# Stage 4 of a four-stage sequence model on one core: query norms inside the exponential, output projection over two tiles, norm bias folded into the first product's bias

## The chip, the cores and the metric

One core of a Trainium2 chip runs the whole program. The metric is the device time of an execution in microseconds (us). The kernel before takes 2695.79 us as the median of three runs (2693.87 to 2695.86).

## The reference, cut to what matters

The program takes 2048 tokens of width 128 through four residual stages. Only the last, a stack of six layers, is touched. The input of that stage is layer-normed first. In each layer, shift_tokens moves the upper 64 features one token on.

```python
def attn_layer(x, Wqkv, qs, ksc, Wo):                # 16 heads of 64
    q, k, v = split(x @ Wqkv)
    q = l2norm(q) * qs;  k = l2norm(k) * ksc         # per head
    q, k = rotary(q, scale), rotary(k, 1 / scale)
    out = local_attention(q, k, v)                   # windows of 32, each sees itself and the one before
    return out @ Wo
def local_attention(q, k, v):
    sim = einsum('bhwie,bhwje->bhwij', bq, bk2) * 8.0
    attn = softmax(where(mask, -max, sim))           # 64 columns per row
    return einsum('bhwij,bhwje->bhwie', attn, bv2)
def ffn_layer(x, g, bln, W1, b1, W2, b2):
    xn = (x - mu) / sqrt(var + 1e-5) * g + bln
    a, gate = split(xn @ W1 + b1)                    # 341 columns each
    return a * gelu(gate) @ W2 + b2
for i in range(6):
    x = attn_layer(shift_tokens(x), ...) + x
    x = ffn_layer(shift_tokens(x), ...) + x
```

## The kernel before, in words

Stage 4 works on tiles of 128 tokens: 16 tiles a layer, 96 in six layers. The residual lies transposed in SBUF (features in partitions), in two buffers s4[0] and s4[1]. All data are 32-bit floats.

One loop, `for i in range(last + 2 * G + len(parts))`, is a software pipeline. In each pass it calls the list `steps` in the order written, and each step has a lag: `(mix, 4)` works in pass i on tile i - 4. The engines keep the program's order, because every call goes through `InOrder` (this is why nearly all lines in the profile are L66, the helper's). So in each pass ACT, for instance, runs in this order: the square of Q (sq), the copy of V (vt), the exponential (ex), what the feed-forward step needs, the square of K (sq again), and four copies out of PSUM (qT, kT, pT, oT).

The steps of one tile are these. `project` multiplies by the weights of Q or K into ps (PE) and squares it (ACT). `rotate` makes the two rotary terms rot_a and rot_b out of ps (DVE), `rotate_sum` adds them (POOL), `squares` sums sq by head into ss (DVE). `norms` raises ss to the power -1/2 (POOL, rn: the inverse norms of Q in rn[:, 0] and of K in rn[:, 1]); `normed` multiplies K by its norms (POOL). `turn` transposes Q and K (PE into pt, ACT copies to qT and kT). `scores` makes sc out of a mask and 64 small products (PE). `shift` takes the row maximum mx, subtracts it (DVE, sm) and multiplies by the norms of Q (POOL, sm again). `expo` is the exponential (ACT, ex). `project_v` makes the values (PE into pv, ACT copies to vt, and DMAs on SP's queue spread vt over the windows of vw). `flip` transposes ex (PE into ptp, ACT copies to pT). `weigh` multiplies by the values (PE into po) and divides by the row sum (DVE, rd and o). `turn_o` transposes o (PE into pto, ACT copies to oT), `mix` multiplies by the output weights (PE into px), and `take` adds px to the residual (DVE, two halves of 64 partitions because of the shift).

The feed-forward part works on groups of four tiles (512 columns), cut in seven `parts`, of which a pass runs those with index p = i mod 4 and p + 4: ff_mean with the second of three products ff_up, ff_var with the third, ff_norm with ff_down, and the first ff_up alone. ff_mean makes xc and its square xsq, ff_norm spreads the inverse deviation over PSUM (prb) and normalises, ff_up makes ph (PE), the GELU ge (ACT) and the gated act (DVE).

PSUM is one pool of four buffers of two banks each; `big` hands them out to all of the products named above, and a product waits until the one that had its buffer has been read. The pool `wk` holds twelve SBUF tiles of 128x1024 for sq, rot_b, sm, ex, qT, pT, o and oT.

The exponential and the GELU use different tables on ACT; the compiler puts a table load ahead of an instruction whose table isn't in place.

Of the kernel before, what the change touches and what calls it, by code (L numbers as in the profile page):

```python
# [11 lines left out]
F32 = mybir.dt.float32  # L12
BF16 = mybir.dt.bfloat16
I32 = mybir.dt.int32
AF = mybir.ActivationFunctionType
ALU = mybir.AluOpType
# [3 lines left out]
P = 128  # L20
T = 2048
NT = T // P
# [12 lines left out]
DEPTH = 6  # L35
# [3 lines left out]
NPAIR = HEADS // 2  # L39
WIN = 32  # L40
NWIN = P // WIN
QK_SCALE = 8.0
FFI = 341
FCH = [(0, 128), (128, 128), (256, 85)]
# [6 lines left out]
def _bc(ap, shape):  # L51

    return ap.unsqueeze(len(shape) - 1).to_broadcast(shape)
# [30 lines left out]
class Kernel:  # L84
# [722 lines left out]
    def stage4(self, x3T, out):  # L807
        nc, tc, a = self.nc, self.tc, self.a
        with ExitStack() as ctx:
            self.pools4.append(ctx.enter_context(tc.tile_pool(name="s4w1", bufs=1)))  # L810
            const = ctx.enter_context(tc.tile_pool(name="s4c", bufs=1))
            pool = ctx.enter_context(tc.tile_pool(name="s4", bufs=2))
            pool3 = ctx.enter_context(tc.tile_pool(name="s43", bufs=3))
            wk = ctx.enter_context(tc.tile_pool(name="s4wk", bufs=12))
            psum = ctx.enter_context(tc.tile_pool(name="s4b", bufs=4, space=PSUM))


# [5 lines left out]
            vec = const.tile([P, DEPTH, 9], F32, name="vec4")  # L823
# [29 lines left out]
            for g in range(NG):  # L853
                cols = slice(g * GW, (g + 1) * GW)
                xc = pool.tile([P, GW], F32, name="xc")
                pr = self.norm_columns(xc, x3T[:, cols], mean_w, pool, psum)
# [6 lines left out]
            pe, dve, act, gps, sp = self.pe, self.dve, self.act, self.gps, InOrder(tc, nc.sync)  # L863
            st = [{} for _ in range(DEPTH * NT + 1)]
            ff = [{} for _ in range(DEPTH * NG)]

            def big(name):
                return psum.tile([P, 2, 512], F32, name=name, tag="big")
# [139 lines left out]
            def shift(t):  # L1008
                s_ = st[t]
                sc = s_.pop("sc").rearrange("p h n k -> p (h n) k")  # L1010
                mx = pool.tile([P, HEADS], F32, name="mx4")
                dve.reduce_max(mx, sc, axis=AX.X)
                sm = wk.tile([P, HEADS, 2 * WIN], F32, name="sm", tag="wk")
                dve.tensor_tensor(sm, sc, _bc(mx, [P, HEADS, 2 * WIN]), ALU.subtract)

                gps.tensor_tensor(
                    sm.rearrange("p (h n) k -> p h n k", h=2),
                    sm.rearrange("p (h n) k -> p h n k", h=2),
                    _bc(s_.pop("rn")[:, 0, :].rearrange("p (n h) -> p h n", h=2), [P, 2, NPAIR, 2 * WIN]),
                    ALU.mult,  # L1020
                )
                s_["sm"] = sm

            def expo(t):
                s_ = st[t]
                sm = s_.pop("sm")
                ex = wk.tile([P, NPAIR, 2, 2 * WIN], F32, name="ex4", tag="wk")
                act.activation(
                    ex.rearrange("p n h k -> p h n k"), sm.rearrange("p (h n) k -> p h n k", h=2), AF.Exp
                )  # L1030
                s_["ex"] = ex

            def flip(t):
# [38 lines left out]
            def turn_o(t):  # L1072
                o = st[t].pop("o")
                pt = big("pto4").rearrange("p a (n c) -> p (a n) c", c=P)
                for n in range(NPAIR):
                    pe.transpose(pt[:, n, :], o[:, n].rearrange("p h d -> p (h d)"), self.ident)
                oT = wk.tile([P, NPAIR, P], F32, name="oT", tag="wk")
                act.copy(oT, pt)
                st[t]["oT"] = oT

            def mix(t):
                wo = self.w4[t // NT][1]
                oT = st[t].pop("oT")
                px = big("px4")[:, 0, 0:P]
                for n in range(NPAIR):
                    pe.matmul(px, lhsT=wo[:, n, :], rhs=oT[:, n, :], start=n == 0, stop=n == NPAIR - 1)
                st[t]["px"] = px

            def take(t):
                i, px = t % NT, st[t].pop("px")  # L1090
                for h in range(2):
                    rs = slice(64 * h, 64 * h + 64)
                    cols = slice(i * P + h, (i + 1) * P + h)
                    dve.tensor_tensor(s4[1][rs, cols], s4[0][rs, cols], px[rs], ALU.add)


# [23 lines left out]
            def ff_norm(g):  # L1120
                xc, r, vc = ff[g]["xc"], ff[g].pop("r"), vec[:, g // NG]
                pr = big("prb")[:, 0]
                for j in range(G):
                    pe.matmul(
                        pr[:, j * P : (j + 1) * P], lhsT=r[:, j : j + 1].to_broadcast([P, P]), rhs=self.ident,
                        start=True, stop=True,
                    )
                dve.tensor_tensor(xc, xc, pr, ALU.mult)
                dve.tensor_scalar(xc, xc, vc[:, 0:1], vc[:, 1:2], ALU.mult, ALU.add)

            def ff_up(g, i):
                (c0, cn), xc, vc, w1 = FCH[i], ff[g]["xc"], vec[:, g // NG], self.w4[g // NG][2]
# [13 lines left out]
            def ff_down(g):  # L1146
# [12 lines left out]

            parts = [  # L1160
                ff_mean, ff_var, ff_norm, lambda g: ff_up(g, 0), lambda g: ff_up(g, 1), lambda g: ff_up(g, 2), ff_down
            ]

            def feed_forward(i):
# [6 lines left out]

            steps = [
                (lambda t: project(t, 0), 0), (mix, 4), (lambda t: rotate(t, 0), 0), (take, 4), (scores, 2),
                (lambda t: squares(t, 0), 0), (shift, 2), (normed, 1), (lambda t: rotate_sum(t, 0), 0), (table, -1),
                (project_v, 2), (expo, 2), (weigh, 3), (feed_forward, None),
                (lambda t: project(t, 1), 0), (turn, 1), (lambda t: rotate(t, 1), 0), (lambda t: rotate_sum(t, 1), 0),
                (pass_on, 1), (lambda t: squares(t, 1), 0), (flip, 2), (turn_o, 3), (norms, 0),
            ]
            last = DEPTH * NT
            table(0)  # L1180
            for i in range(last + 2 * G + len(parts)):
                if i % NT == 12 and i // NT + 1 < DEPTH:
                    self.load4(i // NT + 1)
                for step, late in steps:
                    if late is None:
                        step(i)
                    elif 0 <= i - late < last:
                        step(i - late)
# [141 lines left out]
```

## Time and profile before

| | us |
|---|---|
| median of three runs | 2695.79 |
| the profiled execution | 2700.82 |
| its span, first to last instruction | 2699.1 |
| PE, DVE, ACT, POOL busy in the span | 2459.0, 1821.7, 1349.7, 1658.8 |
| PE, DVE, ACT, POOL busy in 1900 to 2200 us | 286.1, 223.7, 168.5, 268.6 |
| exponential of stage 4, 96 of 128x1024, each | 1.057 |
| POOL's multiply of sm by the norms, 96, each | 1.911 |
| px, 1536 matmul records of 128 columns, each | 0.280 |
| table loads on ACT, 133, each | 1.283 |

The profile is of one execution, 5.0 us above the median. A row gives the number of instructions, their busy time and the mean duration of one; a product of 32-bit floats appears as two records. Records of PE overlap their neighbours, so the distance from start to start is the better measure of what a matmul costs. Stage 4 begins at about 900 us. A busy share is an average: it doesn't tell which engine the next step is waiting for.

### The profile page before, as it was taken

Reading aid. Unit: us, or ns where it says so; the run is one execution under the profiler, and the core shown is the slowest. Engines: PE = TensorE matmul, PEld = TensorE weight load, DVE = VectorE, ACT = ScalarE, POOL = GpSimd, SP = SyncE. Lnnn points to the kernel's source line nnn. Section 1 sums busy time; section 2 is a strip of 40 time slices with the busy share of each in tenths; the row PEclk is TensorE's granted clock in tenths of the full one; section 3 lists DMA queues with packets and bytes.
Section 4 is the critical chain, followed back from the end, with each engine's and each line's share of the span. In section 5 each row is a group of like instructions: output and inputs, shape, how many; then the busy total and the mean of one; then the engine's idle time right before and its main releaser. Section 6 shows DMA issues by size and latency. Waiting matters only on the chain.

```text
span 2699.1 us, 85362 instructions
## 1 busy us (share of the span) xinstructions
PE 2459.0 (91%) x37600; PEld 1478.4 (55%) x37600; DVE 1821.7 (67%) x2764; ACT 1349.7 (50%) x1806; POOL 1658.8 (61%) x1011
## 2 busy tenths in 40 slices
PE   3489999999999689999999999999999999999997
PEld 1473333333333366666666666666666666666664
DVE  6766664476642467777777777777777777777774
ACT  1132455544555144555555555555555555556552
POOL 4310000000001599989888888898888988898980
PEclk8689999999999799999999999999999999999999
DMA  2000000000000222233222322232323222222221
GB/s 82 1 1 1 1 1 1 2 1 1 1 1 1 62 65 69 60 88 72 59 66 67 89 58 71 66 87 60 73 62 82 69 66 67 59 60 65 60 59 43
DMA packets 93566, 128.39 MB, mean 48 GB/s; under 512 B 26248, under 2 KB 41104, under 8 KB 93072
## 3 DMA queue, kind: packets, MB, share of 16 engines
q1 hardware_dynamic: 92620, 122.48, 18.6%
q8 instruction: 299, 4.90, 0.8%
q10 hardware_dynamic: 580, 0.46, 0.1%
q14 instruction: 67, 0.55, 0.1%
HBM read 20.35 MB, written 1.05 MB: 8 GB/s over the span
## 4 chain that ended last, share of the span: by engine, by line
PE 63%; DVE 21%; ACT 6%; issue 5%; POOL 4%; SPq 1%; DMA 0%; DVEq 0%; ACTq 0%; POOLq 0%
PE sc L66 17%; PE ps L66 10%; PE av L66 6%; PE pt L66 5%; DVE mx L66 4%; PE py L66 4%; DVE rot_a L66 4%; DVE sm L66 4%; DVE ss L66 4%; PE ph L66 3%; DVE rot_b L66 3%; PE pto L66 3%; PE ptp L66 3%; ACT sq L66 3%; POOL sm L66 2%
## 5 line engine op out<-in xcount | busy, mean ns | idle before, releaser
L66 DVE TENSOR_REDUCE mx<-sc 128x1 f32<-128x512 f32 (+4 forms) x736 | 471.0, 685 | 238.9 <-PE sc L66 234.1
L66 POOL TENSOR_TENSOR rot_a<-rot_a,rot_b 128x1024 f32<-128x1024 f32 x192 | 459.2, 2392 | 144.1 <-DVE rot_b L66 143.9
L66 POOL TENSOR_TENSOR rn<-ss,mhalf 128x32 f32<-128x32 f32 x96 | 523.9, 5457 | 8.0
L66 ACT ACTIVATE ex<-sc 128x512 f32<-128x512 f32 (+3 forms) x640 | 310.0, 531 | 302.4 <-PE sc L66 301.3
L66 PE MATMUL sc<-kT,qT 64*32 64x64 f32 (+2 forms) x13568 | 429.7, 260 | 9.6 <-ACT qT L66 9.3
L66 POOL TENSOR_SCALAR_AFFINE_SELECT ex<-ex 128x512 f32<-128x512 f32 x64 | 40.6, 634 | 628.2 <-ACT ex L66 628.2
L66 DVE TENSOR_TENSOR rot_a<-ps,tab 128x1024 f32<-128x1024 f32 x192 | 235.0, 1224 | 221.9 <-ACT sq L66 205.3
L66 PE MATMUL sc<-qT,kT 32*128 32x512 f32 (+3 forms) x1280 | 369.4, 581 | 2.3 <-DVE qT L66 2.1
L66 PE MATMUL ps<-wqkv,s 128*128 128x512 f32 x768 | 367.8, 602 | 1.5 <-DVE rd L66 1.5
L66 ACT COPY vt<-pv 128x1024 f32<-128x1024 f32 x96 | 97.2, 1013 | 443.4 <-PE pv L66 425.4
L66 PEld LDWEIGHTS sc<-kT,qT 64*32 64x32 f32 (+1 forms) x13568 | 221.5, 113 | 139.1 <-issue 68.9
L66 ACT ACTIVATE sq<-ps 128x1024 f32<-128x1024 f32 x192 | 195.9, 1020 | 101.4 <-PE ps L66 101.4
L66 DVE TENSOR_REDUCE ss<-sq 128x16 f32<-128x1024 f32 x192 | 233.1, 1214 | 2.8
L66 DVE TENSOR_TENSOR rot_b<-ps,tab 128x1024 f32<-128x1024 f32 x192 | 233.0, 1213 | 0.0
L66 PEld LDWEIGHTS pt<-ident,rot_a 128*128 128x128 f32 x1536 | 175.5, 142 | 76.8 <-issue 40.3
L66 PEld LDWEIGHTS px<-oT,wo 128*128 128x128 f32 x1536 | 182.3, 193 | 63.5 <-ACT oT L66 61.4
L66 PEld LDWEIGHTS ps<-wqkv,s 128*128 128x128 f32 x768 | 138.6, 191 | 141.5 <-issue 136.7
L66 ACT ACTIVATE ex<-sm 128x1024 f32<-128x1024 f32 x96 | 101.5, 1057 | 221.2 <-POOL sm L66 221.2
L66 PE MATMUL pt<-ident,rot_a 128*128 128x128 f32 x1536 | 188.3, 275 | 23.3 <-POOL rot_a L66 23.1
L66 POOL TENSOR_TENSOR sm<-sm,rn 128x1024 f32<-128x1024 f32 x96 | 183.5, 1911 | 40.6 <-DVE rd L66 18.7
L66 DVE SCALAR_TENSOR_TENSOR act<-ph,vec,ge 128x512 f32<-128x512 f32 (+1 forms) x72 | 54.0, 750 | 220.1 <-ACT ge L66 220.0
L66 PE MATMUL px<-oT,wo 128*128 128x128 f32 x1536 | 194.9, 280 | 6.7 <-ACT oT L66 6.7
(212 smaller groups left out, 4014.2 us busy)
## 6 DMA issues: line engine op xcount, KB each, us to landing
vw<-vt SPq DMA_DIRECT2D x1524, 65.0 KB, 2.0
wqkv<-in_L_ffn_Wqkv SPq DMA_DIRECT2D x18, 512.0 KB, 5.1
wo<-in_L_ffn_Wo SPq DMA_DIRECT2D x6, 512.0 KB, 4.7
w<-in_L_ffn_W SPq DMA_DIRECT2D x6, 341.0 KB, 3.3
x<-in_L_attn_hidden_states SPq DMA_DIRECT2D x4, 256.0 KB, 4.3
rot<-in_rot SPq DMA_DIRECT2D x1, 1024.0 KB
out<-ot SPq DMA_DIRECT2D x4, 256.0 KB, 2.2
w<-in_L_ffn_W SPq DMA_DIRECT2D x12, 64.0 KB, 2.6
```

The lines of the kernel that those rows point to most:

```text
L66: return self._tc.keep_in_program_order(call(*args, **kw))
```

## The change

`shift` no longer multiplies by the norms of Q. `expo` becomes 16 instructions, one for each head, on 64 columns each, and each gives its head's column of rn as the scale of the exponential: exp(rn * (sc - mx)). rn is positive, so the maximum stays the maximum.

`turn_o` copies into one half of an oT that two tiles share, out of a pool of its own with two buffers. `mix` and `take` do nothing for an even tile; for an odd one they work on both (256 columns).

`ff_norm` multiplies by g and by prb in one step and leaves out the bias. A new function, `ff_bias`, called once in each layer ahead of the steps of pass i with i mod 16 = 6, makes the product of that bias with W1 (six products with one column) and adds it to b1. `wk` goes from twelve tiles to ten.

```diff
-            wk = ctx.enter_context(tc.tile_pool(name="s4wk", bufs=12))
+            wk = ctx.enter_context(tc.tile_pool(name="s4wk", bufs=10))
...
                 dve.tensor_tensor(sm, sc, _bc(mx, [P, HEADS, 2 * WIN]), ALU.subtract)
-
-                gps.tensor_tensor(
-                    sm.rearrange("p (h n) k -> p h n k", h=2),
-                    sm.rearrange("p (h n) k -> p h n k", h=2),
-                    _bc(s_.pop("rn")[:, 0, :].rearrange("p (n h) -> p h n", h=2), [P, 2, NPAIR, 2 * WIN]),
-                    ALU.mult,
-                )
                 s_["sm"] = sm
...
-                sm = s_.pop("sm")
+                sm, rn = s_.pop("sm"), s_.pop("rn")
                 ex = wk.tile([P, NPAIR, 2, 2 * WIN], F32, name="ex4", tag="wk")
-                act.activation(
-                    ex.rearrange("p n h k -> p h n k"), sm.rearrange("p (h n) k -> p h n k", h=2), AF.Exp
-                )
+
+                for n in range(NPAIR):
+                    for h in range(2):
+                        act.activation(
+                            ex[:, n, h, :], sm[:, h * NPAIR + n, :], AF.Exp, scale=rn[:, 0, 2 * n + h : 2 * n + h + 1]
+                        )
...
-                oT = wk.tile([P, NPAIR, P], F32, name="oT", tag="wk")
-                act.copy(oT, pt)
-                st[t]["oT"] = oT
+                if t % 2 == 0:
+                    st[t + 1]["oT"] = pool.tile([P, NPAIR, 2, P], F32, name="oT")
+                oT = st[t + 1 - t % 2]["oT"]
+                act.copy(oT[:, :, t % 2], pt)
...
             def mix(t):
+                if t % 2 == 0:
+                    return
...
-                px = big("px4")[:, 0, 0:P]
+                px = big("px4")[:, 0, 0 : 2 * P]
                 for n in range(NPAIR):
-                    pe.matmul(px, lhsT=wo[:, n, :], rhs=oT[:, n, :], start=n == 0, stop=n == NPAIR - 1)
+                    pe.matmul(
+                        px, lhsT=wo[:, n, :], rhs=oT[:, n].rearrange("p j c -> p (j c)"), start=n == 0, stop=n == NPAIR - 1
+                    )
...
             def take(t):
-                i, px = t % NT, st[t].pop("px")
+                if t % 2 == 0:
+                    return
+                i, px = t % NT - 1, st[t].pop("px")
...
-                    cols = slice(i * P + h, (i + 1) * P + h)
+                    cols = slice(i * P + h, (i + 2) * P + h)
...
-                dve.tensor_tensor(xc, xc, pr, ALU.mult)
-                dve.tensor_scalar(xc, xc, vc[:, 0:1], vc[:, 1:2], ALU.mult, ALU.add)
+
+                dve.scalar_tensor_tensor(xc, xc, vc[:, 0:1], pr, ALU.mult, ALU.mult)
+
+            def ff_bias(l):
+                w1, vc = self.w4[l][2], vec[:, l]
+                pb = big("pbias")[:, 0, 0:6]
+                for h in range(2):
+                    for i, (c0, cn) in enumerate(FCH):
+                        pe.matmul(
+                            pb[0:cn, 3 * h + i : 3 * h + i + 1], lhsT=w1[:, h * FFI + c0 : h * FFI + c0 + cn],
+                            rhs=vc[:, 1:2], start=True, stop=True,
+                        )
+                for i, (_, cn) in enumerate(FCH):
+                    dve.tensor_tensor(vc[0:cn, 3 + i : 9 : 3], vc[0:cn, 3 + i : 9 : 3], pb[0:cn, i:6:3], ALU.add)
...
+                if i % NT == 6 and i // NT < DEPTH:
+                    ff_bias(i // NT)
```

## The prediction

> **What bounds the kernel now.** I read the page first: the last two thirds of the span (stage 4) have PE at 9 tenths, POOL at 8 to 9, DVE at 7, ACT at 5. That looks like a kernel bound by PE, with ACT half idle. The waits by engine (window 1500 to 2500 us, about 55 tiles) show where ACT's idle time sits:
>
> ```profile
> ACT vt L66 <- PE pv L66: 240.8, 52, 5.2
> ACT ex L66 <- POOL sm L66: 120.8, 55, 3.3
> PEld px L66 <- ACT oT L66: 33.3, 55, 0.7
> ```
>
> PE's own waits are small, and ACT waits twice in each tile: for pv, and for POOL's multiply. Next the timeline of one pass of the loop, ACT alone, in a pass that also runs a feed-forward product (columns: start, time taken, instruction, idle time before it):
>
> ```profile
> 2044.29 1.03 ACT L66 ACTIVATE sq<-ps 128x1024 f32<-128x1024 f32 x1 [0.24 <-PE ps L66]
> 2049.95 1.01 ACT L66 COPY vt<-pv 128x1024 f32<-128x1024 f32 x1 [4.63 <-PE pv L66]
> 2050.98 1.28 ACT L66 ACT_TABLE_LOAD   x1
> 2054.06 1.06 ACT L66 ACTIVATE ex<-sm 128x1024 f32<-128x1024 f32 x1 [1.79 <-POOL sm L66]
> 2055.02 0.61 ACT L66 ACTIVATE xsq<-xc 128x512 f32<-128x512 f32 x1
> 2055.65 1.28 ACT L66 ACT_TABLE_LOAD   x1
> 2056.94 0.69 ACT L66 ACTIVATE ge<-ph,vec 128x512 f32<-128x512 f32 x1
> 2057.53 1.02 ACT L66 ACTIVATE sq<-ps 128x1024 f32<-128x1024 f32 x1
> 2058.43 1.01 ACT L66 COPY qT<-pt 128x1024 f32<-128x1024 f32 x1
> 2059.32 1.04 ACT L66 COPY kT<-pt 128x1024 f32<-128x1024 f32 x1
> 2060.23 1.04 ACT L66 COPY pT<-ptp 128x1024 f32<-128x1024 f32 x1
> 2061.13 1.06 ACT L66 COPY oT<-pto 128x1024 f32<-128x1024 f32 x1
> 2062.44 1.02 ACT L66 ACTIVATE sq<-ps 128x1024 f32<-128x1024 f32 x1 [0.25 <-PE ps L66]
> ```
>
> The reader is to see that from ex to oT ACT has no idle time, and that the next sq comes only 0.25 us after it could. Between the first sq and ex lies DVE: rot_a, rot_b, take, ss, mx, sm in one string, sm ending 7.75 us after the first sq began. So there is a ring, sq, DVE's string, POOL's multiply, ex, ACT's string, sq, that is as long as PE's work (18.15 us here). PE and this ring bound the stage together; whatever lengthens the ring shows in full, whatever shortens only one of the two shows hardly at all.
>
> **What the Trainium skill says.** "ScalarE: Activation LUTs", section What ACT_TABLE_LOAD costs: an instruction costs 186 ns + 0.833 ns a column, a pointer operand adds about 93 ns, neighbours overlap by about 93 ns, a table load takes 1283 ns. The trace agrees: loads 1283 ns; ge (bias by pointer, 512 columns) 687 ns against 590 ns of a copy of that size; ge begins 0.58 us before the next, 0.1 less than it takes. "TensorE: Matmul & The Clock Gate", section Part 1: The HAM clock gate: PE's activity is judged in free windows of 3.4 us, and after an idle one PE runs at half clock. In the trace's tail, where PE has gaps of 0.55 and 1.76 us close together, the same px takes 3.45 us in place of 1.95 to 2.05:
>
> ```profile
> 2638.71 3.45 PE L66 MATMUL px<-oT,wo 128*128 128x128 f32 x16 [1.76 <-ACT oT L66]
> ```
>
> **The change, part by part.** Times are counted from S, the start of the pass's first sq. I name passes by i mod 4: a (2: norm and down), b (3: up 0), c (0: mean and up 1), d (1: variance and up 2). The timeline from 2008 us has them as a 18.56, b 17.69, c 18.15, d 17.70, together 72.1.
>
> *The exponentials.* One ex of 1057 ns becomes 16 of 128x64 with a scale by pointer. The trace has no such row. From its rows: 1057 less 960 columns at 0.833 is 257 ns, plus 97 for the pointer (687 against 590) is 354 ns; neighbours overlap by about 0.1 (ex starts 0.96 before xsq). So about 0.25 us each, 4.0 us for 16. Bounds: 0.354 without overlap (5.7 us); 0.12 if start and pointer both hide, worked out from stage 3, where a second 128-column exponential adds only 0.175 us (0.107 of columns, 0.068 fixed):
>
> ```profile
> 664.90 0.45 ACT L66 ACTIVATE ex<-sc 128x128 f32<-128x128 f32 x2 [1.40 <-PE sc L66]
> L66 ACT ACTIVATE ex<-sc 128x128 f32<-128x128 f32 x64 | 14.3, 275 | 29.3 <-PE sc L66 29.1
> ```
>
> I take 0.25, because a pointer showed its full price behind ge.
>
> *POOL's multiply* (1.91 us) leaves the ring: ex may start when sm ends, not 2.0 later. But part of this is lost. In the built order the wait for sm now stands ahead of the table load on ACT, where before the load had no wait and ran while POOL multiplied. In c, d and a, which load the exponential's table, 1.28 us become visible; b loads none. So c's first ex starts at S+8.5, against S+9.8. Behind that wait stand, in ACT's order, the 16 exponentials, ge, sq and the four copies, and for these wait act and ptp (ge), DVE's next rot_a (sq), pto (qT), ps (kT) and px (oT).
>
> *Two tiles at once.* px of 16 matmul records at 0.11 us becomes, in odd passes (b, d), 16 at 0.215 (a 512-column record of ps is 0.43), 3.44 us, and nothing in a and c. PE's sum is the same but for 0.07 us a tile. The placing is not: in b and d, sc and pv come 1.65 later and the vt copy, ahead of ex on ACT, ends at S+8.43 instead of S+6.67. DVE's take is gone in a and c (0.6 us, sm ends S+7.12) and 0.83 in b and d (sm ends S+8.13, take waiting for px until S+3.5).
>
> *The walk round the ring*, with ACT's own spacings (ex to load 4.1, load 1.30, ge 0.58, sq 0.91, qT 0.89, kT 0.90, pT 0.90, oT 1.07; xsq 0.63 more in c):
> - a: first ex S+8.47, sq at S+12.47 (ps has been ready since S+11.5), next S at 17.15: 1.41 less.
> - b: ex S+8.45, next S at 19.1: 1.41 more.
> - c: ex S+8.47, next S at 19.65: 1.50 more.
> - d: vt S+8.43, load, ex S+9.75, next S at 20.4: 2.70 more.
>
> Sum +4.2 us in four passes. In each, ps for the next S needs the kT copy and ends within 0.1 of oT, so PE gives no relief. Products of the feed-forward lie beside attention in 22 such rounds (passes 11 to 97): 22 x 4.2 = 92. The nine passes before them go from 16.25 to a mean of 16.45: +2.
>
> *Half clock.* In c PE has finished pt at S+12.35, and ptp must take the buffer that act frees after ge: S+16.0. An idle stretch of 3.6 us is new; before it was 0.2. At half clock one window costs up to 1.7 us of PE work, and ps is on the path. Bounds 0 and 37 us over 22 rounds (1.7 each); I take 1.0 each, 22.
>
> *The bias product.* Six one-column products a layer, 12 records at 0.11 to 0.12 (pvar's 8 take 0.9), ahead of ps at i mod 16 = 6, where ps is on the path: 1.4 x 6 = 8. They also hold a PSUM buffer until three small DVE additions, which run while DVE waits for sq. *The norm*: xc's two DVE steps (0.68 and 1.89) become one of 0.75. Worth nothing: DVE then idles 1.1 us before rot_a for sq. *Buffers 12 to 10*: oT has its own pair now; the new waits in the built order (qT and pT copies for POOL's sums) are for sums that end at S+12 at the latest, before those copies. Nothing; SP's DMAs are unchanged.
>
> Sum 92 + 2 + 22 + 8 = 124, onto the profiled execution's 2700.8: 2825. The median stands 5 below that execution, so **2820**.
>
> **The rivals.**
> - *Cheap exponentials, faster.* The place is the 16 instructions between sm and ge. At 0.12 us they take 1.94: b, c, d gain 2.06 each on my walk and a 1.0 (ps at S+11.5 then ends last): 4.2 - 7.2 = -3.0 a round, -65, with 10 for bias and first passes and no half clock: -55, 2641. It decides from 0.173 us each downwards (3.7 us a round to be found in b, c and d: 1.23 less than 4.0). For it: the 0.068 of stage 3. Against: ge's pointer shows 0.1, and SBUF sources cost 37 ns more than PSUM ones (1057 against 1020).
> - *Exponentials without overlap.* 5.66 us: 1.66 more in all four passes, 146 more: 2966. Against: every back-to-back pair on ACT overlaps by 0.1.
> - *Half clock spreads.* The window after c's stall falls on d's long px: 1.7 more a round, 37: 2857. For: the tail's px. Against: d's px comes over 3 us after the stall.
> - *PE alone bounds*, and the ring's time is covered: then only 0.07 x 96 = 7 us of px less 8 of bias: 2697. Against: the next sq waits only 0.25 us.
>
> **How the numbers follow.** About 0.2% is what a measurement of this kernel can tell from no change. My walk 0.66, half clock spreading 0.14, no overlap 0.08, cheap exponentials 0.09, PE alone 0.03. The range, 2745 (exponentials near 0.2 us, no half clock) to 2900 (0.30 us with half clock), holds the first two and leaves out the last three, 0.20 together. Faster 0.09, same 0.03, slower 0.88.
>
> **What would show it.** In the changed profile: ex rows of 128x64 near 350 ns starting 0.25 apart; a table load directly after sm in c, d and a; no idle time on ACT from there to oT; PE waiting for act before ptp, by 3 us in c; passes b and d longer than a; clock below 1.0 inside stage 4. It is wrong if ACT still waits before ge, or if the exponentials stand 0.17 apart or closer.

## The result and the profile after

The changed kernel takes 2812.65 us (median of four runs, 2808.81 to 2814.19) against 2695.82 in the same comparison: 116.8 us more, ratio 1.0431 with a 95% interval of 1.0413 to 1.0449. The forecast was 2820, in a range of 2745 to 2900.

The waits of the changed kernel, in the window 1500 to 2500 us that was shown of before (columns: waiting engine and tile, whom it waited for, us in total, times, longest):

```profile
ACT vt L66 <- PE pv L66: 215.5, 49, 6.3
PE ptp L66 <- DVE act L66: 60.4, 31, 3.4
ACT L66 <- DVE sm L66: 57.1, 24, 2.7
ACT sq L66 <- PE ps L66: 30.8, 52, 1.9
```

ACT's wait for POOL's sm is gone. In its place a nameless ACT instruction, the table load, waits for DVE's sm, and PE waits 60 us for act, where it waited 4 us in the same window of the kernel before. The load's wait occurs 24 times in some 13 rounds of four passes, twice a round: in the passes a and c. In the page's chain of work that ended last ACT's share rose from 6% to 20%, POOL's fell from 4% to 1%.

The same pass as before on ACT, c, in its timeline (start, time taken, instruction, idle time before it; the copies qT, kT and pT, which follow the second sq without a gap, are left out):

```profile
2034.54 1.03 ACT L66 ACTIVATE sq<-ps 128x1024 f32<-128x1024 f32 x1 [0.30 <-PE ps L66]
2038.24 1.01 ACT L66 COPY vt<-pv 128x1024 f32<-128x1024 f32 x1 [2.67 <-PE pv L66]
2041.62 1.28 ACT L66 ACT_TABLE_LOAD   x1 [2.36 <-DVE sm L66]
2042.91 3.93 ACT L66 ACTIVATE ex<-sm,rn 128x64 f32<-128x64 f32 x16
2046.75 0.62 ACT L66 ACTIVATE xsq<-xc 128x512 f32<-128x512 f32 x1
2047.38 1.28 ACT L66 ACT_TABLE_LOAD   x1
2048.68 0.69 ACT L66 ACTIVATE ge<-ph,vec 128x512 f32<-128x512 f32 x1
2049.26 1.01 ACT L66 ACTIVATE sq<-ps 128x1024 f32<-128x1024 f32 x1
2053.24 1.01 ACT L66 COPY oT<-pto 128x1024 f32<-128x1024 f32 x1 [0.23 <-PE pto L66]
2055.70 1.02 ACT L66 ACTIVATE sq<-ps 128x1024 f32<-128x1024 f32 x1 [1.45 <-PE ps L66]
```

The load follows sm and is seen in full. The 16 exponentials stand from 2042.91 to 2046.75, 0.24 apart. From the load to the pT copy ACT has no gap.

In pass d the load is seen in full too, but for another reason. The vt copy ends only at 8.17 us after the pass began (median), behind sm at 8.01, because the long px stands ahead of pv on PE; the load follows vt directly, with no wait between them:

```profile
2062.85 1.01 ACT L66 COPY vt<-pv 128x1024 f32<-128x1024 f32 x1 [6.13 <-PE pv L66]
2063.88 1.28 ACT L66 ACT_TABLE_LOAD   x1
```

At the end of pass c sq waits 1.45 us for ps, and PE's timeline of the same stretch says why:

```profile
2045.14 1.91 PE L66 MATMUL pt<-ident,rot_a 128*128 128x128 f32 x16
2050.20 1.22 PE L66 MATMUL ptp<-ident,ex 128*128 128x128 f32 x8 [3.16 <-DVE act L66]
2051.23 1.97 PE L66 MATMUL pto<-ident,o 128*128 128x128 f32 x8
2052.99 2.61 PE L66 MATMUL ps<-wqkv,s 128*128 128x512 f32 x4
```

After 3.16 us without work, pto takes 1.97 us and ps 2.61, where the next pass has 1.09 and 1.96. The table of windows, with one row for each of the passes b, c, d, a (columns: stretch, its length, busy time of PE, PEld, DVE, ACT, POOL with instructions, PE's granted clock, DMA share, GB/s), shows the clock below 1.0 in c alone. So it is in all 21 rounds: it fell in 16 of the passes c and in none of a, b and d.

```profile
2015.54:2034.54 19.00, 18.34 (x324) 12.19 (x323) 12.83 (x15) 12.44 (x25) 13.91 (x8) 1.00 0.25 59
2034.54:2055.70 21.16, 17.31 (x310) 10.90 (x309) 12.27 (x14) 14.40 (x28) 15.42 (x9) 0.92 0.25 59
2055.70:2075.95 20.25, 19.06 (x332) 12.84 (x330) 12.89 (x16) 13.76 (x26) 13.38 (x8) 1.00 0.24 54
2075.95:2093.10 17.15, 16.36 (x317) 10.69 (x316) 13.09 (x15) 11.77 (x24) 13.90 (x8) 1.00 0.11 30
```

Below, a pass is measured from its first sq to the next pass's, over the 21 rounds of passes 11 to 94, and its mean is given:

| kernel | a | b | c | d | round |
|---|---|---|---|---|---|
| before | 18.79 | 17.71 | 18.17 | 17.72 | 72.4 |
| changed | 17.17 | 19.08 | 20.87 | 20.57 | 77.7 |
| exponentials alone, 12 buffers | 18.83 | 18.57 | 19.24 | 18.77 | 75.4 |
| exponentials alone, 13 buffers | 18.69 | 18.63 | 21.27 | 19.92 | 78.5 |
| pairing alone | 17.16 | 18.11 | 18.02 | 18.82 | 72.1 |
| changed, early load | 17.14 | 18.98 | 18.94 | 19.27 | 74.3 |
| changed, doubled transposes in c | 17.16 | 19.04 | 19.71 | 20.67 | 76.6 |
| Q normed before the transpose | 18.78 | 17.48 | 17.79 | 18.04 | 72.1 |

Changed less before is 5.3 us a round, in 21 rounds 111 of the 112 us by which the two profiled executions differ: nearly the whole difference lies in these passes.

### The profile page after: what moved, and what is told of

The parts are those of the page before. It is cut to its first block, busy times and chain, and to the rows that moved or that the text cites. A ratio compares the mean times of both kernels' runs of the same rounds, so it can differ in the third digit from the quotient of the medians.

```text
span 2811.2 us, 85235 instructions
## 1 busy us (share of the span) xinstructions
PE 2503.1 (89%) x36904; PEld 1474.5 (52%) x36904; DVE 1779.6 (63%) x2662; ACT 1621.2 (58%) x3246; POOL 1473.6 (52%) x915
## 4 chain that ended last, share of the span: by engine, by line
PE 57%; ACT 20%; DVE 16%; issue 4%; POOL 1%; SPq 1%; DMA 1%; ACTq 0%; DVEq 0%; POOLq 0%
PE sc L66 18%; ACT ex L66 9%; PE ps L66 8%; PE av L66 6%; PE px L66 5%; ACT L66 4%; PE pto L66 4%; PE py L66 4%; PE ptp L66 3%; DVE mx L66 3%; DVE sm L66 3%; PE pv L66 2%; DVE ss L66 2%; DVE rot_a L66 2%; ACT sq L66 2%
## 5 line engine op out<-in xcount | busy, mean ns | idle before, releaser
L66 POOL TENSOR_TENSOR rot_a<-rot_a,rot_b 128x1024 f32<-128x1024 f32 x192 | 453.5, 2362 | 455.8 <-DVE rot_b L66 442.3
L66 ACT ACTIVATE ex<-sm,rn 128x64 f32<-128x64 f32 x1536 | 377.3, 334 | 14.7 <-DVE sm L66 9.0
L66 PE MATMUL ps<-wqkv,s 128*128 128x512 f32 x768 | 380.7, 620 | 2.5 <-ACT qT L66 1.5
L66 PE MATMUL ptp<-ident,ex 128*128 128x128 f32 x768 | 112.1, 290 | 102.8 <-DVE act L66 101.3
L66 PEld LDWEIGHTS po<-vw,pT 64*32 64x32 f32 x12288 | 136.9, 105 | 102.7 <-issue 96.1
```

The costliest lines, as they stand in the source:

```text
L66: return self._tc.keep_in_program_order(call(*args, **kw))
```

## The experiments

All times are medians; each stands beside runs of the kernel before on the same chip (2695.4 to 2697.4).

**The parts, one at a time.**

*The exponentials alone* (`x_exp`), on the kernel before (the lines of the diff are shortened):

```diff
-                gps.tensor_tensor(sm, sm, _bc(rn of Q), ALU.mult)
...
-                act.activation(ex, sm, AF.Exp)
+                for n in range(NPAIR):
+                    for h in range(2):
+                        act.activation(ex[:, n, h, :], sm[:, h * NPAIR + n, :], AF.Exp, scale=rn[:, 0, 2 * n + h : 2 * n + h + 1])
```

> The kernel before with the exponential part of the change alone (POOL's multiply gone, 16 scaled exponentials; one tile at a time, two-step norm, twelve buffers). Theory (the ring through ACT bounds): sm ends S+7.75 as before, the table load then follows it in a, c and d (ex from S+9.1), in b ex starts at S+7.8; 16 exponentials at 0.24 us take 3.83. a stays 18.56 (ps ends only at S+13.4), b +0.9, c +2.05, d +2.2, sum 5.15 in four passes, 22 rounds 113, first passes +8, some half clock in c on top: 2815 to 2835. Rival (pairing makes the loss, exponentials are covered): within 20 us of before.

Measured: 2762.21, ratio 1.0236 (1.0210 to 1.0262), 65 us more than before. Both expectations missed. The exponentials do cost, but about half of what I expected: b, c and d take 0.9 to 1.1 us more and a nothing, which is what the ring gains when 2.8 us more of exponentials come in and 1.95 of POOL's multiply go out. The timeline of its pass c shows why it isn't more:

```profile
2013.82 1.01 ACT L66 COPY vt<-pv 128x1024 f32<-128x1024 f32 x1 [4.58 <-PE pv L66]
2014.84 1.28 ACT L66 ACT_TABLE_LOAD   x1
2016.14 3.93 ACT L66 ACTIVATE ex<-sm,rn 128x64 f32<-128x64 f32 x16
```

The load runs directly behind vt, with no wait for sm. So the exposed load of the changed kernel doesn't come from taking POOL's multiply away alone, as I had thought. In the built order of the changed kernel, ex waits for two things, sm and an earlier instruction of ACT itself; one of the two becomes a wait of its own, and the load is put between that and ex. Here, with twelve buffers and ten allocations a pass, ex has nothing to wait for but sm, and the load is all but free (ex starts 0.1 us later than in b, which has no load). The semaphores in the traces agree in all 21 rounds: in the changed kernel a wait for DVE's semaphore stands ahead of the load and ex itself waits for ACT's; in `x_exp` nothing stands ahead of the load and ex waits for DVE's alone. Whether there is a second wait can depend on the buffer of the pool that ex gets, and on what used it before.

*That reading tested* (`x_exp13`, `x_exp10`): the same kernel with another number of wk buffers.

```diff
-            wk = ctx.enter_context(tc.tile_pool(name="s4wk", bufs=12))
+            wk = ctx.enter_context(tc.tile_pool(name="s4wk", bufs=13))   # x_exp10: bufs=10
```

> The exponentials alone, as in the earlier run of them (2762, 12 wk buffers), with 13 wk buffers. In the built order the table load of the exponential then stands behind the wait for sm in all passes that load it; with 12 it stands ahead of that wait. Theory (which buffer ex gets decides whether a second wait, and with it the load, lands behind sm): c and d +1.25 each, a 0 (ps ends last there), 22 rounds: +55 to +65 with some half clock, 2815 to 2830, slower with more memory. Rival (the load is exposed in the full change because ten buffers are too few): no slower than with 12, 2762.

> The exponentials alone with 10 wk buffers, the number of the full change, at ten allocations a pass. The load stands behind the wait for sm here too. Theory: as with 13 buffers, 2815 to 2830. Rival (buffers run short as well): more than 10 us above the run with 13.

Measured: 2828.55 with 13, ratio 1.0497 (1.0475 to 1.0519), and 2828.10 with 10, ratio 1.0493 (1.0471 to 1.0515). One buffer more costs 66 us, and ten cost the same as thirteen, so it isn't scarcity. In both ex has a second wait (with 13 for POOL's semaphore, with 10 for ACT's), and a wait for DVE's stands ahead of the load in a, c and d. The 13-buffer kernel's pass c:

```profile
2046.10 1.01 ACT L66 COPY vt<-pv 128x1024 f32<-128x1024 f32 x1 [4.57 <-PE pv L66]
2048.36 1.28 ACT L66 ACT_TABLE_LOAD   x1 [1.24 <-DVE sm L66]
```

The load now waits 1.24 us for sm. In the table, d takes 1.15 more and c 2.03 more, the load plus half clock (in 12 of the 21 passes c the clock fell); a and b are as with 12.

*The pairing alone* (`x_pair`): on the kernel before, mix, take and turn_o as in the change, with ten wk buffers.

> The kernel before with the pairing of two tiles alone (mix, take, own oT buffers, ten wk buffers; POOL multiplies as before, two-step norm). Theory: in odd passes px of 3.44 us makes PE the bound, b +0.65 and d +1.5; in even passes without px a -1.8 and c -0.7; sum -0.35 in four passes, about -10: 2675 to 2700. Rival (the uneven passes are what costs in the full change): +40 or more.

Measured: 2698.62, ratio 1.0000 (0.9989 to 1.0011). As expected, a is 1.6 shorter, d 1.1 and b 0.4 longer (c falls by 0.2 only, not by 0.7): the passes become uneven and their sum stays.

*The folded norm bias alone* (`x_fold`): ff_norm and ff_bias as in the change.

> The kernel before with the folded norm bias alone (one DVE step in place of two, six one-column products and three additions a layer). Theory: DVE's saved 1.8 us lie in time in which DVE waits for sq; the product costs 1.3 to 1.4 us on the path in each layer: +8, 2700 to 2706. Rival (DVE's long step of 1.89 us is on the path in pass a): -20 or so, 2675.

Measured: 2703.01, ratio 1.0023 (1.0012 to 1.0034): 6 us, the bias product. DVE's shorter step brings nothing.

**Terms of the changed kernel, taken out one at a time.**

*The load early* (`y_load`): one exponential of a constant column ahead of the vt copy makes the compiler put the table load there, where ACT waits for pv.

```diff
+            tiny = const.tile([P, 2], F32, name="tiny")
+            nc.vector.memset(tiny, 0.0)
...
+                act.activation(tiny[:, 1:2], tiny[:, 0:1], AF.Exp)
                 vt, old = vts[t % 2], vts[1 - t % 2]
```

> The changed kernel with one exponential of a single constant column ahead of each vt copy on ACT, so that the exponential's table is loaded while ACT waits for pv, and not between sm and the 16 exponentials. Theory (the exposed load is on the ring in a, c and d): a -0.75 (then ps ends last, at S+11.45), c -1.25, d -1.3, some of the half clock in c too: 70 to 85 us less than the changed kernel, 2728 to 2745. Rival (the load only fills time that the pairing leaves): within 15 us of the changed kernel.

Measured: 2741.30, ratio 1.0176 (1.0156 to 1.0195), 71 us less than the changed kernel.

```profile
2075.17 1.02 ACT L66 ACTIVATE sq<-ps 128x1024 f32<-128x1024 f32 x1 [0.31 <-PE ps L66]
2076.21 1.28 ACT L66 ACT_TABLE_LOAD   x1
2077.51 0.20 ACT L66 ACTIVATE tiny<-tiny 128x1 f32<-128x1 f32 x1
2078.87 1.01 ACT L66 COPY vt<-pv 128x1024 f32<-128x1024 f32 x1 [1.16 <-PE pv L66]
2082.26 3.93 ACT L66 ACTIVATE ex<-sm,rn 128x64 f32<-128x64 f32 x16 [2.39 <-DVE sm L66]
```

In this pass c ex waits for sm alone; 7.1 us after the pass began, against 8.4 in the changed kernel.

*Eight buffers* (`y_wk8`): `bufs=10` becomes `bufs=8`.

> The changed kernel with 8 wk buffers in place of 10. In the built order the load then stands ahead of the wait for sm in passes a and c and behind it in d. Theory: a -0.75, c -1.25 and less half clock, d the same: 42 to 60 us less than the changed kernel, 2752 to 2771. Rival (fewer buffers make the ring wait for buffers): slower than the changed kernel.

Measured: 2758.16, ratio 1.0235 (1.0211 to 1.0259), 54 us less than the changed kernel, with no other edit. Pass c falls to 18.37 and a to 16.90; d doesn't fall (20.71): there vt ends behind sm, so the load is on the path whatever ex waits for.

*A warm PE* (`y_warm`):

```diff
-                    for n in range(NPAIR):
-                        pe.transpose(pn[:, n, :], rq[:, n * P : (n + 1) * P], self.ident)
+                    for _ in range(2 if t % G == 3 else 1):
+                        for n in range(NPAIR):
+                            pe.transpose(pn[:, n, :], rq[:, n * P : (n + 1) * P], self.ident)
```

> The changed kernel with the 16 transposes of Q and K done twice in pass c, into the same buffers: 1.75 us more work for PE, laid into the stretch in which it waits 3.2 us for act. Theory (what pass c takes over my walk is half clock after that stretch): with a shorter gap the clock stays up, c falls from 20.9 to 19.7, some 25 us less than the changed kernel, 2780 to 2792. Rival (c's extra time is waiting, not clock): no gain, or a loss of up to 1.75 x 22 = 38.

Measured: 2790.29, ratio 1.0355 (1.0334 to 1.0377), 22 us less than the changed kernel with more work. PE's timeline:

```profile
2030.92 3.66 PE L66 MATMUL pt<-ident,rot_a 128*128 128x128 f32 x32
2036.00 1.09 PE L66 MATMUL ptp<-ident,ex 128*128 128x128 f32 x8 [1.42 <-DVE act L66]
2037.03 1.09 PE L66 MATMUL pto<-ident,o 128*128 128x128 f32 x8
2037.96 1.97 PE L66 MATMUL ps<-wqkv,s 128*128 128x512 f32 x4
```

The gap is 1.42 in place of 3.16, and pto and ps have their full speed; the clock is 1.00 in all 21 passes c. Pass c falls from 20.87 to 19.71, the others stay. So the clock was 1.2 us of each c.

*Both* (`y_both`):

> The changed kernel with the early table load and with the doubled transposes in pass c. Theory: the two terms add where the clock still fell: 2720 to 2740, and what is left over the kernel before is the 16 exponentials in b, c and d, less the pass a that pairing shortens. Rival (pairing costs by itself once the exponentials are there): 2760 or more, near the run with the exponentials alone.

Measured: 2743.78, ratio 1.0183 (1.0165 to 1.0202): not below the early load alone. With the load gone, the gap in c is shorter; the doubled transposes hold the clock at 1.00 (0.99 without), but delay c about as much as they save. That the two add was wrong.

*No pointer* (`y_noscale`): `scale=1.0`, leaving out the norms of Q.

> The changed kernel with a constant scale of 1.0 in the 16 exponentials; it leaves the norms of Q out. Theory (a pointer costs 0.1 us of spacing, as behind ge): 0.14 instead of 0.24 apart, 1.5 less in b, c and d and 0.75 in a, 5.3 in four passes: some 115 us less than the changed kernel, 2690 to 2715. Rival (the pointer is read behind the instruction before): same time as the changed kernel.

Measured: 2696.67, ratio 0.9999 (0.9986 to 1.0011), 116 us less than the changed kernel. The groups of ACT between 1500 and 2500 us, without the pointer and then in the changed kernel (count | busy us, mean ns | idle before):

```profile
L66 ACT ACTIVATE ex<-sm 128x64 f32<-128x64 f32 x871 | 133.2, 241 | 0.4
```

```profile
L66 ACT ACTIVATE ex<-sm,rn 128x64 f32<-128x64 f32 x822 | 202.0, 334 | 0.5
```

A pointer costs 93 ns, and none of it hides: sixteen times the distance from start to start is 2.35 us without it and 3.84 with it.

**The multiply off the ring without its price** (`x_qnorm`): on the kernel before, Q is multiplied by its norms where K is.

```diff
+                rn = st[t].pop("rn")
+                for s in range(2):
-                v = st[t]["rq", 1].rearrange("p (h d) -> p h d", d=HD)
-                gps.tensor_tensor(v, v, _bc(st[t]["rn"][:, 1, :], [P, HEADS, HD]), ALU.mult)
+                    v = st[t]["rq", s].rearrange("p (h d) -> p h d", d=HD)
+                    gps.tensor_tensor(v, v, _bc(rn[:, s, :], [P, HEADS, HD]), ALU.mult)
...
-                gps.tensor_tensor(sm, sm, _bc(rn of Q), ALU.mult)      # shortened
```

> The kernel before with POOL's multiply moved off the ring and no other edit: Q is multiplied by its norms where K is, before the transpose, so ex follows sm directly with one instruction. Same instructions on every engine. Theory (PE's work and the ring are equally long, so taking 1.95 us from the ring alone gives only what PE leaves): passes fall to PE's own length, a about 18.0, b 16.5, c 17.2, d 17.1, some 3 us in four passes, 40 to 75 us faster: 2620 to 2655. Rival A (PE alone bounds): no more than 10 us faster. Rival B (the ring alone bounds): 1.95 in every pass, 180 us faster.

Measured: 2682.93, ratio 0.9951 (0.9935 to 0.9966), 14 us less than before. It is faster than both kernels, but my size was wrong and rival A is nearly right. Its waits name the bound:

```profile
ACT sq L66 <- PE ps L66: 104.5, 84, 5.9
```

sq now waits for PE. In the table, b gains 0.2 and c 0.4, a nothing, and d, where I gave PE a length of 17.1, takes 18.04 (median 17.73). In c the ring wasn't shortened by 1.95: in all 21 rounds the load stands behind sm there, and ex starts 9.11 us after the pass began, against 9.76 before and 7.8 in the other passes.

*The same in the full change* (`z_all`): pairing and folded norm stay, one exponential a tile.

> The changed kernel with the norms of Q multiplied in on POOL before the transpose and one exponential a tile; pairing and folded norm stay. Theory (pairing and the folded norm are worth about nothing where PE bounds, and the moved multiply some 14 us): 2675 to 2695. Rival (with the ring shortened, pairing's saved PE time of 0.07 us a tile and the shorter even passes show): below 2670.

Measured: 2680.22, ratio 0.9941 (0.9922 to 0.9960): as fast as `x_qnorm` within the intervals, and 132 us faster than the changed kernel.

## Why the prediction was right, point by point

- **The ring.** Right, and the reason for the result. The walk gave a 17.15, b 19.1, c 19.65 before clock and d 20.4; the medians are 17.15, 19.00, 19.69 (with the clock kept up by `y_warm`) and 20.27.
- **The exponentials.** 0.25 us apart forecast, 0.24 measured; 354 ns a piece forecast, 334 measured. The Trainium skill's figures ("ScalarE: Activation LUTs", What ACT_TABLE_LOAD costs) give 186 + 93 + 53 (64 columns) - 93 = 239 ns as an estimate, and the runs agree. The faster rival needed 0.173 or less; `y_noscale`, at 0.147, comes out level with the kernel before. By the rival's own sum it should have been faster by some 28 us (an estimate: 1.65 less in b, c and d and 1.0 in a). PE ends last there: in b and d it is idle for 0.2 us a pass or less.
- **The table load.** Its wait, its place and its price were right (`y_load`: 71 us with the half clock that goes with it); the place had been read from the built order. Its cause was wrong in a and c and right in d. The prediction said that removing POOL's multiply exposes it, and priced "Buffers 12 to 10" at nothing; `x_exp` without the multiply hides it, and `x_exp13` exposes it by one buffer more. What decides in a and c is whether ex has a second wait beside sm. The number of buffers can change that, but isn't all: in `x_qnorm`, with twelve buffers, the load is exposed in c and not in a and d, and what adds the second wait there stays open. In d pairing exposes it, through the late vt copy, as the walk had it ("vt S+8.43, load, ex S+9.75"). Whether the changed kernel with twelve buffers would hide it in a and c wasn't tried: beside the oT pair they don't fit.
- **Pairing.** Alone worth nothing, as in the walk. Once the exponentials lengthen the ring it helps: with the load exposed in both, the change (2812.65) is 15 us below the exponentials alone (`x_exp10`); with it hidden in both, `y_load` is 21 us below `x_exp`. Short passes a pay for it.
- **Half clock.** 22 us forecast (1.0 a round), 22 measured. That the number fits so well is partly luck, since 1.0 was picked between 0 and 1.7. It did not spread to d. The idle window of 3.4 us from which the prediction argued isn't needed in full: of 21 passes c the clock fell in 16 where the gap was 3.16 us (median), in 12 at 2.26 (`x_exp13`), in 7 at 1.88 (`y_load`), in one at 1.82 (`y_wk8`) and in none at 1.42 (`y_warm`).
- **The bias product.** 8 us forecast, 6 measured alone; the norm's DVE step nothing, as forecast.
- **PE's own length.** The prediction took PE and the ring for equally long. That holds if PE's short waits for DVE are counted in. My later expectation for `x_qnorm` put PE at about 3 us a round below the ring, and it is not. Its lengths (18.0, 16.5, 17.2, 17.1) are close to PE's work without its idle time (18.0, 16.4, 17.5, 17.0 before); the step that failed was to leave that idle time out. It stays at 0.8 to 1.0 us a pass when the ring is shorter, most of it in a, c and d a wait for DVE's rd (0.6 to 0.75).

## What to carry to other kernels

Where two engines' chains are equally long, adding to either shows nearly in full and taking from one shows hardly at all: the 16 exponentials in place of POOL's multiply made the ring 0.9 us longer and cost 65 us (0.9 to 1.1 in three passes of four), while taking POOL's 1.95 us off the ring (0.65 in c) gave 14. Sixteen small instructions with a pointer cost 0.24 us each for 0.05 us of columns (an estimate from 1057 ns for 1024 columns and 241 for 64), so a per-head factor is better multiplied where a whole tile passes anyway. Look at what stands ahead of a table load in the built order: a second wait on the instruction behind it, here changed by the turn of a buffer pool, can put 1.28 us on the path; so can an instruction ahead of it that ends late, here vt in d.

## What the runs showed of the hardware that I had not expected

Useless work can shorten a kernel: 1.75 us of repeated transposes in a stretch where PE waited brought 22 us, because PE kept its clock. In the pass c that is shown a gap of 3.16 us was followed by pto and ps at 1.97 and 2.61 us, a gap of 1.42 at the same place by 1.09 and 1.97. The length of the gap alone doesn't decide it: after the same gap of 3.16 us the clock held in five of the 21 passes c.
